# Expert chunks four at a time: evidence products in five blocks, PSUM banks by number

## The chip, the cores and the metric

One Trainium2 chip; the kernel runs on one of its cores, in one launch. The metric is device time in microseconds (us), as the median of several runs. Engines are named as the profile names them: PE (TensorE, matrix products), DVE (VectorE), ACT (ScalarE), POOL (GpSimd) and SP (SyncE, which here only issues transfers).

## The reference, cut to what matters

Eight samples of 512 tokens with 256 features. Everything is float32.

```python
nx = layer_norm(x) * ln_gamma + ln_beta                  # (8, 512, 256)
k, v = context @ Wk, context @ Wv                         # (8, 64, 256)
weights = softmax(nx @ Wq @ k.T / 16)                     # (8, 512, 64)
evidence = weights @ v                                    # (8, 512, 256)
combined = concat([nx, evidence, anchor])                 # (8, 512, 768)
probs = softmax(combined @ router_W + router_b)           # 3 experts
h = silu(combined @ e_w1[e] + e_b1[e])                    # 512 wide, each e
routed = sum_e probs_e * (h_e @ e_w2[e] + e_b2[e])
g = sigmoid(silu(combined @ gate_w1 + gate_b1) @ gate_w2 + gate_b2)
out = x + g * (routed @ out_w + out_b)
```

## The kernel before

The samples are worked on in four pairs, `j` = 0 to 3. Tokens lie on the free side: an activation is a tile of 128 features by 512 tokens, and one such tile fills one PSUM bank.

**The first layer.** Its 14 chunks of 128 outputs (12 of three experts, 2 of the gate) form seven groups of two chunks, `GROUPS`: group 0 is the gate's, 1 and 2 are expert 0's, 3 and 4 expert 1's, 5 and 6 expert 2's. For each group the four outputs of a 2x2 problem (two chunks times the two samples of the pair) are computed with seven products in place of eight, on sums and differences of the operands (`ws`, `T`, `combine_x`). They gather in three banks, U, Y and Z. By the numbers that the changed code gives them they are: 1 opens U; 2 goes to Y; 5 and then 3 go to Z; 6, 7 and 4 go to U. Between them partial sums have to be taken out: U after 1 and after 6 and Z after 5 by an ACT copy, U after 7 and Y after 2 by a DVE addition. A product that adds to a bank waits for the copy or addition that reads it. `silu` on ACT makes the four outputs; the last of them read U and Z when all is in.

**The evidence's part.** The term `evidence @ W` is added as `vw^T wT` with a contraction of only 64 rows (64 context positions). Two such products, one for each sample, use the upper and the lower 64 rows of PE. `evidence(j, n)` issues a block of them: one for U of group n-2, one for Z of n-1, one each for Y and Z of group n.

**Weighing.** Each expert chunk is multiplied by its router probability on DVE (`weigh`, line 714, tile `pb`, four per group), and one subtraction per group prepares the second layer (line 711). They are put in a list, `late`, and `weigh` takes a fixed number off it at fixed places.

**The second layer and the gate** are in `outputs(j, steps)`: the gate's seven products (`ps_gu`, `ps_gy`, `ps_gz`), then seven runs of six products over the chunks, with the subtractions of line 843, the bias sums (ACT 848, DVE 852) and the final sums (872 to 875). Steps of the next pair are put between them: transposes of its tokens, scores and softmax, `value_weights`, the router. One small detour matters here: a 3-row piece of `vw` is written to DRAM (`vrd`, line 331, POOL's queue) and read back on all partitions (`vr`, line 333); `router_logits` (lines 570 to 583, DVE) multiplies with it.

In pair 0 the preparation of the weights is spread over the first layer as well: `anchor_rows` and `anchor_columns` (biases from the condition), `second_bias`, and for every expert `transpose_second` (DVE, line 402), `second_layer` (PE, line 410, the product of e_w2 and out_w) and `combine_second` (POOL).

The order on every engine is written out by hand (`manual_schedule`): each queue runs in the order in which the code issues, and `put` places the steps. PSUM's eight banks come from four pools: two banks for U, one for Y, two for Z and three (`misc`) that rotate for everything else.

Of the kernel before, what the change touches and what calls it, by code (L numbers as in the profile page):

```python
# [16 lines left out]
def kernel(  # L17
# [74 lines left out]
    ps_x = ctx.enter_context(tc.tile_pool(name="ps_x", bufs=2, space=PSUM))  # L92
    ps_y = ctx.enter_context(tc.tile_pool(name="ps_y", bufs=1, space=PSUM))
    ps_z = ctx.enter_context(tc.tile_pool(name="ps_z", bufs=2, space=PSUM))
    ps_m = ctx.enter_context(tc.tile_pool(name="ps_m", bufs=3, space=PSUM))

    def misc(name):
        return ps_m.tile([P, 512], F32, tag="m", name=name)

    def bank(pool, name):  # L100
        return pool.tile([P, 512], F32, tag="b", name=name)
# [136 lines left out]
    def either(name):  # L238
        turn[0] += 1
        return bank((ps_x, ps_z)[turn[0] % 2], name)  # L240
# [400 lines left out]

    GROUPS = (NE // 2, *range(NE // 2))
    U, Z, Y = {}, {}, {}
# [5 lines left out]
    def take_banks(j, n):  # L649
        Y[n], Z[n] = bank(ps_y, f"ps_y_{j}_{n}"), bank(ps_z, f"ps_z_{j}_{n}")  # L650

    def evidence(j, n, start=True):

        wT, vw = S["wT", j], S["vw", j]
        todo = []
        if n - 2 in U:
            todo.append((U[n - 2], 2 * GROUPS[n - 2] + 1, 0, False))
        if n - 1 in Z:  # L660
            todo.append((Z[n - 1], 2 * GROUPS[n - 1], 1, False))
        if n < len(GROUPS):
            if n:
                take_banks(j, n)
            todo.append((Y[n], 2 * GROUPS[n], 0, start))
            todo.append((Z[n], 2 * GROUPS[n] + 1, 1, start))
        for ps, c, i, first in todo:
            half = slice(i * CT, (i + 1) * CT)
            product(ps, vw[half, c * P : (c + 1) * P], wT[half, :], start=first)
# [5 lines left out]
    def silu(j, n, i, d, src):  # L675
        c = 2 * GROUPS[n] + d
        nc.scalar.activation(  # L677
            chunk(n, i, d), src, AF.Silu, bias=abias[:, c, 2 * j + i : 2 * j + i + 1]
        )

    def add_silu(j, n, i, d, part, more):
        h = chunk(n, i, d)
        nc.vector.tensor_tensor(h, more, part, ALU.add)  # L683
        silu(j, n, i, d, h)

    def fourth(j, n):
        c = 2 * GROUPS[n]
        product(U[n], w1[:, 1, (c + 1) * P : (c + 2) * P], S["T", j][:, 2, :])
# [3 lines left out]

    late = []

    def weigh(j, n, most=8):


        for m, d, i in ((n - 1, 1, 0), (n, 0, 0), (n, 0, 1), (n, 1, 1)):
            if 0 < m < len(GROUPS):
                late.append((m, d, i))  # L700
        if 0 < n < len(GROUPS):
            late.append((n, None, None))
        if ("pb", j) in S and (j or n > 2):
            weigh_late(j, most)

    def weigh_late(j, most):
        for m, d, i in late[:most]:
            q = GROUPS[m]
            if d is None:
                b12 = hidden(j, q, 0, 1)  # L710
                nc.vector.tensor_tensor(b12, b12, hidden(j, q, 0, 0), ALU.subtract)
            else:
                h = hidden(j, q, d, i)
                nc.vector.tensor_tensor(h, h, S["pb", j][:, i, 2 * q // RC, :], ALU.mult)  # L714
        del late[:most]

    def first_layer(j, n, steps, last_steps):
        q = GROUPS[n]
        c, g = 2 * q, 2 * q // RC
        if c % RC == 0:  # L720
            for i in range(2):
                S["h", i, g] = h_tile(i, g, f"h_{2 * j + i}_{g}")
        A, Bx = S["nxT", 2 * j], S["nxT", 2 * j + 1]
        t1, t2, t3 = S["T", j][:, 0, :], S["T", j][:, 1, :], Bx[:, 0, :]
        ca, cb = chunk(n, 0, 0), chunk(n, 1, 0)
        U[n] = bank(ps_x, f"ps_u_{j}_{n}")
        product(U[n], w1[:, 0, c * P : (c + 1) * P], A[:, 0, :], start=True)
        first = j == n == 0
        if n == 0:
            take_banks(j, 0)  # L730
        if first:
            anchor_columns(E, either)
            anchor_columns(0, either)
            transpose_w(0)
        elif n == 0:
            evidence(j, 0)
        nc.scalar.copy(ca, U[n])  # L737
        if n:
            silu(j, n - 1, 1, 1, chunk(n - 1, 1, 1))
        product(Y[n], w1[:, 1, c * P : (c + 1) * P], A[:, 1, :], start=first)  # L740
        product(Z[n], ws[:, S1, q, :], t1, start=first)
        if first:
            evidence(j, 0, start=False)
        z = work.tile([P, T], F32, tag="z", name=f"z_{j}_{n}", bufs=1)
        nc.scalar.copy(z, Z[n])
        add_silu(j, n, 0, 0, Y.pop(n), ca)
        for step in steps:
            step()
        if n == 1:
            b12 = S["h", 1, E][:, 0, :]  # L750
            nc.vector.tensor_tensor(b12, b12, S["h", 0, E][:, 0, :], ALU.subtract)
        weigh(j, n - 1)
        if n:
            fourth(j, n - 1)
        product(U[n], ws[:, S2, q, :], t2)
        nc.scalar.copy(cb, U[n])
        product(Z[n], ws[:, S4, q, :], Bx[:, 1, :])
        evidence(j, n + 1)
        if n:
            silu(j, n - 1, 0, 1, U.pop(n - 1))  # L760
        add_silu(j, n, 1, 0, Z.pop(n), cb)
        product(U[n], w1[:, 0, (c + 1) * P : (c + 2) * P], t3)
        nc.vector.tensor_tensor(chunk(n, 1, 1), z, U[n], ALU.add)  # L763
        for step in last_steps:
            step()

    def finish_first_layer(j):
        n = len(GROUPS) - 1
        fourth(j, n)
        evidence(j, n + 2)  # L770
        silu(j, n, 0, 1, U.pop(n))

    def outputs(j, steps):
# [7 lines left out]
        silu(j, len(GROUPS) - 1, 1, 1, chunk(len(GROUPS) - 1, 1, 1))  # L781
        weigh(j, len(GROUPS) - 1, 99)
# [4 lines left out]
        def scratch_x(tag, bufs=1):  # L787
            return work.tile([P, T], F32, tag=tag, name=f"g_{tag}_{j}", bufs=bufs)

        def minus(dst, p, m):  # L790
            nc.vector.tensor_tensor(dst, p, m, ALU.subtract)
# [7 lines left out]
        t2, t3, t4 = scratch_x("z"), scratch_x("yb", 2), scratch_x("yb", 2)  # L799
        g1, g2, g22 = scratch_x("r11"), scratch_x("r12"), scratch_x("r22")  # L800
        y, z, u = (misc(f"ps_g{n}_{j}") for n in "yzu")
        product(u, gw[0][0], b11, start=True)
        nc.scalar.copy(g1, u)
        product(z, gw2s[:, S1, :], b12, start=True)
        nc.scalar.copy(g22, z)
        minus(t2, b22, b12)
        minus(t3, t2, b11)
        minus(t4, b21, t2)
        finish_first_layer(j)
# [9 lines left out]
        weigh(j, len(GROUPS), 99)  # L819
# [98 lines left out]
        u, y, z = (bank(p, f"ps_{n}2_{j}") for p, n in ((ps_x, "u"), (ps_y, "y"), (ps_z, "z")))  # L918
# [44 lines left out]
        y = bank(ps_z, "ps_y3")  # L963
# [5 lines left out]
    with tc.manual_schedule(engines=None):  # L969
# [56 lines left out]
        for j in range(NP):  # L1026


            within, ending, between = {}, {}, {}
# [4 lines left out]
            if j == 0:  # L1034
                put(within, 0, value_weights, 0, 1)
                put(ending, 0, router_logits, 0)
                put(within, 1, router_logits, 1)
                put(within, 1, anchor_rows, 1)
                put(within, 1, load_second, 1)
                put(within, 1, second_bias)  # L1040
                for b in range(2):
                    put(within, 2, router_exp, b)
                    put(ending, 2, router, b)
                put(within, 2, anchor_columns, 1)
                put(within, 2, load_second, 2)
                put(within, 2, transpose_second, 0)
                put(ending, 2, second_layer, 0)
                put(ending, 2, spread_probabilities, 0)
                put(ending, 2, combine_second, 0)
                put(within, 3, anchor_rows, 2)  # L1050
                put(within, 3, transpose_second, 1)
                put(ending, 3, second_layer, 1)
                put(ending, 3, combine_second, 1)
                put(ending, 3, weigh_late, 0, 5)
                put(within, 4, anchor_columns, 2)
                put(within, 4, transpose_second, 2)
                put(ending, 4, second_layer, 2)
                put(ending, 4, combine_second, 2)
            if j:
                put(ending, 0, spread_probabilities, j)  # L1060
            put(within, 1 + (j == 0), value_weights, j, 2)
            put(within, 4, load_x_blocks, 2 * j)
            put(within, 6, load_x_blocks, 2 * j + 1)
            if j + 1 < NP:
# [5 lines left out]
                for i in range(2):  # L1070
                    put(within, 3, deviation, j + 1, i)
# [62 lines left out]
```

## Time and profile before

| | |
|---|---|
| median of 3 runs | 488.87 us (488.67 to 489.21) |
| the profiled execution's own time | 489.28 us |
| its span, first to last instruction | 487.5 us |
| mean granted PE clock | 1.00 |
| DVE busy | 349.1 us (72%) |
| ACT busy | 219.1 us (45%) |
| PE's longest wait for another engine after the set-up | 0.87 us (line 647 for DVE line 763, at 54.5 us) |

The profile lists instructions by line of the kernel, with the tiles they write and read (numbers left out: `ps_u` is U of every group). One float32 product shows as two MATMUL records. PE's records are pipelined and overlap: the time of a product is the distance between starts, not the duration of a record. In the timeline "x2" merges neighbours of the same kind, and what stands in brackets is the idle time before the instruction and what ended it.

### The profile page before, as it was taken

Reading aid. Unit: us, or ns where it says so; the run is one execution under the profiler, and the core shown is the slowest. Engines: PE = TensorE matmul, PEld = TensorE weight load, DVE = VectorE, ACT = ScalarE, POOL = GpSimd, SP = SyncE. Lnnn points to the kernel's source line nnn. Section 1 sums busy time; section 2 is a strip of 40 time slices with the busy share of each in tenths; the row PEclk is TensorE's granted clock in tenths of the full one; section 3 lists DMA queues with packets and bytes.
Section 4 is the critical chain, followed back from the end, with each engine's and each line's share of the span. In section 5 each row is a group of like instructions: output and inputs, shape, how many; then the busy total and the mean of one; then the engine's idle time right before and its main releaser. Section 6 shows DMA issues by size and latency. Waiting matters only on the chain.

```text
span 487.5 us, 4704 instructions
## 1 busy us (share of the span) xinstructions
PE 481.2 (99%) x1451; PEld 222.5 (46%) x1451; DVE 349.1 (72%) x649; ACT 219.1 (45%) x391; POOL 77.2 (16%) x96
## 2 busy tenths in 40 slices
PE   8999999999999999999999999999999999999997
PEld 7744355535544434335544343434554343433454
DVE  2855748887879476878869575878879645668782
ACT  3463573468120648467210547567311455556000
POOL 5327032200242100000062200000042200000010
PEclk9999999999999999999999999999999999999999
DMA  9987331512002740612002740432002560000013
GB/s 283 377 110 144 57 131 44 108 22 44 0 16 43 163 142 0 143 30 43 1 17 43 158 144 1 118 56 44 2 16 43 81 180 0 0 0 2 0 19 68
DMA packets 118121, 35.27 MB, mean 72 GB/s; under 512 B 104733, under 2 KB 115089, under 8 KB 117585
## 3 DMA queue, kind: packets, MB, share of 16 engines
q1 hardware_dynamic: 114736, 27.02, 26.4%
q0 software_dynamic: 1472, 7.18, 4.3%
q10 hardware_dynamic: 1888, 0.79, 0.6%
q8 instruction: 11, 0.18, 0.2%
q14 instruction: 14, 0.11, 0.1%
HBM read 27.57 MB, written 7.40 MB: 72 GB/s over the span
## 4 chain that ended last, share of the span: by engine, by line
PE 84%; DMA 6%; ACT 3%; DVE 3%; issue 2%; POOL 1%; DVEq 0%; ACTq 0%; POOLq 0%
PE ps_u L647 39%; PE ps_z L647 18%; PE ps_y L647 12%; PE ps_vw L625 4%; PE ps_gu L647 3%; DMA w<-in_L_xcond_e_w_dram 2%; PE ps_s L525 2%; PE ps_w2o L410 2%; DMA vr<-vrd 2%; PE ps_gz L647 1%; DMA w<-in_L_xcond_gate_w_dram 1%; DVE h L843 1%; ACT h L677 1%; PE ps_gy L647 1%; DMA scr_w<-in_L_xcond_Wk_dram 1%
## 5 line engine op out<-in xcount | busy, mean ns | idle before, releaser
L677 ACT ACTIVATE h<-h,abias 128x512 f32<-128x512 f32 x84 | 60.7, 723 | 28.2 <-DVE h L683 25.9
L647 PE MATMUL ps_u<-h,w2o 128*128 128x512 f32 x144 | 63.8, 592 | 0.0
L714 DVE TENSOR_TENSOR h<-h,pb 128x512 f32<-128x512 f32 x96 | 60.0, 683 | 0.0
L647 PE MATMUL ps_u<-nxT,w 128*128 128x512 f32 x112 | 57.8, 621 | 0.3
L647 PE MATMUL ps_z<-wT,vw 64*128 64x512 f32 x112 | 56.5, 619 | 0.0
L647 PEld LDWEIGHTS ps_u<-h,w2o 128*128 128x128 f32 x144 | 27.4, 190 | 34.0 <-issue 33.9
L647 PE MATMUL ps_z<-h,w2s 128*128 128x512 f32 x96 | 42.6, 593 | 0.2 <-DVE r L858 0.2
L875 POOL TENSOR_TENSOR yb<-yb,xb 128x512 f32<-128x512 f32 x14 | 21.8, 1555 | 129.2 <-DVE yb L874 124.9
L683 DVE TENSOR_TENSOR h<-h,ps_y 128x512 f32<-128x512 f32 x28 | 19.2, 687 | 28.6 <-PE ps_y L647 23.0
L683 DVE TENSOR_TENSOR h<-h,ps_z 128x512 f32<-128x512 f32 x28 | 19.1, 684 | 20.1 <-PE ps_z L647 12.8
L647 PEld LDWEIGHTS ps_u<-nxT,w 128*128 128x128 f32 x112 | 18.4, 189 | 32.7 <-issue 17.2
L763 DVE TENSOR_TENSOR h<-z,ps_u 128x512 f32<-128x512 f32 x28 | 19.2, 687 | 19.4 <-PE ps_u L647 19.4
L677 ACT ACTIVATE h<-ps_u,abias 128x512 f32<-128x512 f32 x28 | 19.2, 687 | 30.1 <-PE ps_z L647 25.2
L647 PE MATMUL ps_u<-wT,vw 64*128 64x512 f32 x56 | 31.4, 641 | 0.0
L843 DVE TENSOR_TENSOR h<-h,h 128x1024 f32<-128x1024 f32 x24 | 31.0, 1347 | 0.0
L737 ACT COPY h<-ps_u 128x512 f32<-128x512 f32 x28 | 16.4, 584 | 31.8 <-PE ps_u L647 18.1
L647 PE MATMUL ps_u<-T,w 128*128 128x512 f32 x56 | 28.9, 598 | 0.9 <-DVE h L763 0.9
L647 PE MATMUL ps_y<-wT,vw 64*128 64x512 f32 x56 | 29.3, 604 | 0.0
L647 PE MATMUL ps_y<-nxT,w 128*128 128x512 f32 x56 | 28.9, 598 | 0.0
L647 PE MATMUL ps_z<-nxT,ws 128*128 128x512 f32 x56 | 28.9, 597 | 0.0
L647 PE MATMUL ps_u<-T,ws 128*128 128x512 f32 x56 | 28.6, 592 | 0.0
L647 PE MATMUL ps_z<-T,ws 128*128 128x512 f32 x56 | 28.6, 592 | 0.0
(197 smaller groups left out, 764.4 us busy)
## 6 DMA issues: line engine op xcount, KB each, us to landing
pb<-pd POOLq DMA_DIRECT2D x4, 1536.0 KB, 6.5
x<-in_x_dram SPq DMA_DIRECT2D x8, 512.0 KB, 5.5
xb<-in_x_dram SPq DMA_DIRECT2D x64, 64.0 KB, 2.5
out_dram<-yb SPq DMA_DIRECT2D x56, 64.0 KB, 2.0
w<-in_L_xcond_e_w_dram SPq DMA_DIRECT2D x6, 512.0 KB, 9.4
xd<-x SPq DMA_DIRECT2D x6, 512.0 KB, 2.8
xg<-xd SPq DMA_DIRECT2D x48, 64.0 KB, 2.5
scr_wa<-in_L_xcond_e_w_dram SPq DMA_DIRECT2D x3, 512.0 KB, 5.5
```

What stands on the lines that cost most here:

```text
L410: nc.tensor.matmul(ps[:, d * H : (d + 1) * H], w2T[:, k, (i + d) * P : (i + d + 1) * P], ow_sb[:, k, :], start=(k == 0), stop=(k == KH - 1),)
L525: nc.tensor.matmul(ps[:, t, :], nxT[:, k, t * P : (t + 1) * P], mr[:, k, b, :], start=(k == 0), stop=(k == KH - 1),)
L625: nc.tensor.matmul(ps, vT[:, k, j * 2 * CT : (j + 1) * 2 * CT], w1[:, KH + k, n0:n1], start=(k == 0), stop=(k == KH - 1),)
L647: nc.tensor.matmul(ps, lhsT, rhs, start=start, stop=True, skip_group_check=not start)
L677: nc.scalar.activation(chunk(n, i, d), src, AF.Silu, bias=abias[:, c, 2 * j + i : 2 * j + i + 1])
L683: nc.vector.tensor_tensor(h, more, part, ALU.add)
L714: nc.vector.tensor_tensor(h, h, S["pb", j][:, i, 2 * q // RC, :], ALU.mult)
L737: nc.scalar.copy(ca, U[n])
L763: nc.vector.tensor_tensor(chunk(n, 1, 1), z, U[n], ALU.add)
L843: nc.vector.tensor_tensor(d, p, m, ALU.subtract)
L875: nc.gpsimd.tensor_tensor(yb, yb, S["xb", 2 * j + row][:, i, :], ALU.add)
```

## The change

The gate's group is done first by itself (`gate_layer`), then each expert's two groups together (`expert_layer`), with their products alternating. The evidence's products are issued in one block at the end of each of these, and one for the gate's group at its start: five blocks for each pair of samples. The banks are taken by number; `spares` says which banks `misc` may rotate over at a place. The partial sums wait in the `h` chunks themselves. The gate's differences (`gate_differences`, before in `outputs`) move into expert 2's layer, and the steps of `put` get new places.

```diff
-    ps_x ... bufs=2, ps_y ... bufs=1, ps_z ... bufs=2, ps_m ... bufs=3
+    psum = ctx.enter_context(tc.tile_pool(name="psum", bufs=1, space=PSUM))
+    def bank(i, name):
+        return psum.tile([P, 512], F32, tag=f"b{i}", name=name)
     def misc(name):
+        spare.append(spare.pop(0))
+        return bank(spare[-1], name)
+    spares(4, 6, 7)
...
+    PAIRS = [(1 + 2 * e, 2 + 2 * e) for e in range(E)]
+    Z_BANKS = ((5, 7), (0, 2), (5, 7))
+    def fresh(j, e):
+        for n, y, z in zip(PAIRS[e], (4, 6), Z_BANKS[e]):
+            Y[n], Z[n] = bank(y, ...), bank(z, ...)
...
+    def gate_layer(j, steps):
...
+        U[n] = bank(0, f"ps_u_{j}_{n}")
+        nx_product(j, n, 1, True)
+        Y[n], Z[n] = bank(5, f"ps_y_{j}_{n}"), bank(2, f"ps_z_{j}_{n}")
...
+            evidence(j, ((n, True),))
+        spares(3, 1)
+        keep_part(n, 0, 0, U[n])
+        nx_product(j, n, 5, first)
...
+        keep_part(n, 1, 1, Z[n])
+        nx_product(j, n, 6)
+        keep_part(n, 1, 0, U[n])
+        if not first:
+            nx_product(j, n, 2)
...
+        fresh(j, 0)
+        evidence(j, [(m, True) for m in PAIRS[0]] + [(n, False)])
...
+    def expert_layer(j, e, steps):
+        a, b = PAIRS[e]
...
+        if e:
+            finish_groups(j, PAIRS[e - 1])
...
+        U[a] = bank(1, f"ps_u_{j}_{a}")
+        nx_product(j, a, 1, True)
+        keep_part(a, 0, 0, U[a])
...
+        U[b] = bank(3, f"ps_u_{j}_{b}")
+        nx_product(j, b, 1, True)
...
+        finish_odd(j, PAIRS[e - 1] if e else (0,))
+        if e > 1 or e and j:
+            weigh(j, 5)
+        spares(*Z_BANKS[1 - e % 2])
+        nx_product(j, a, 2)
+        add(a, 0, 0, Y[a])
+        nx_product(j, a, 5)
+        keep_part(a, 1, 1, Z[a])
+        run("A")
+        nx_product(j, a, 6)
...
+        nx_product(j, b, 6)
...
+        nx_product(j, b, 2)
...
+        nx_product(j, b, 5)
...
+        spares(*Z_BANKS[1 - e % 2], 4, 6)
+        run("B")
+        for n in (a, b):
+            nx_product(j, n, 7)
+            add(n, 1, 1, U[n])
...
+        if e:
+            weigh(j, 6)
+        run("C")
...
+        for n in (a, b):
+            nx_product(j, n, 3)
+        run("D")
+        for n in (a, b):
+            nx_product(j, n, 4)
+        if e + 1 < E:
+            fresh(j, e + 1)
+            evidence(j, [(m, False) for m in (a, b)] + [(m, True) for m in PAIRS[e + 1]])
+        else:
+            evidence(j, [(m, False) for m in (a, b)])
...
     def outputs(j, steps):
-        silu(j, len(GROUPS) - 1, 1, 1, chunk(len(GROUPS) - 1, 1, 1))
-        weigh(j, len(GROUPS) - 1, 99)
...
+        u, z, y = (bank(i, f"ps_g{n}_{j}") for n, i in (("u", 0), ("z", 2), ("y", 4)))
         product(u, gw[0][0], b11, start=True)
+        product(z, gw2s[:, S1, :], b12, start=True)
+        finish_groups(j, PAIRS[-1])
         nc.scalar.copy(g1, u)
+        finish_odd(j, PAIRS[-1])
         nc.scalar.copy(g22, z)
-        minus(t2, b22, b12)
-        minus(t3, t2, b11)
-        minus(t4, b21, t2)
-        finish_first_layer(j)
+        spares(6, 7, 4)
...
         run("begin")
-        weigh(j, len(GROUPS), 99)
+        weigh(j, 99)
...
-        u, y, z = (bank(p, ...) for p, n in ((ps_x, "u"), (ps_y, "y"), (ps_z, "z")))
+        u, y, z = (bank(i, f"ps_{n}2_{j}") for i, n in ((1, "u"), (3, "y"), (5, "z")))
...
+                put(within, (0, "A"), router_logits, 1)
+                put(within, (0, "A"), anchor_rows, 1)
+                put(within, (0, "A"), load_second, 1)
+                put(within, (0, "B"), second_bias)
...
+                put(within, (1, "A"), transpose_second, 1)
+                put(within, (1, "B"), second_layer, 1)
+                put(within, (1, "B"), combine_second, 1)
+                put(within, (1, "C"), anchor_columns, 2)
+                put(within, (1, "C"), transpose_second, 2)
+                put(within, (1, "D"), second_layer, 2)
+                put(within, (1, "D"), combine_second, 2)
-                put(ending, 3, weigh_late, 0, 5)
...
+            put(within, (0, "C" if j == 0 else "B"), value_weights, j, 2)
+            put(within, (1, "C"), load_x_blocks, 2 * j)
+            put(within, (2, "A"), gate_differences, j)
+            put(within, (2, "C"), load_x_blocks, 2 * j + 1)
...
+                put(within, (0, "A"), statistics, b0, 0, NT)
+                put(within, (0, "C" if j else "D"), statistics, b1, 0, NT)
+                put(within, (1, "C"), deviation, j + 1, i)       # for i in 0, 1
+                put(within, (1, "D"), normalize, b0)
+                put(within, (2, "C"), normalize, b1)
+                put(within, (2, "C"), store_x, b1)
```

In the new functions `keep_part` is the ACT copy of a partial sum into its `h` chunk, `add` the DVE addition, `finish_groups` the SiLU from U and the addition of Z for two groups, `finish_odd` the SiLUs after that addition. `nx_product(j, n, which)` issues the product with that number.

## The prediction

> **What bounds the kernel now.** I read the page's busy times first, then PE's timeline around an evidence block, then the other engines' timelines at the places where a step moves.
>
> ```profile
> PE 481.2 (99%) x1451; PEld 222.5 (46%) x1451; DVE 349.1 (72%) x649; ACT 219.1 (45%) x391; POOL 77.2 (16%) x96
> ```
>
> PE is busy for 481 of 487.5 us: PE's order sets the time, a product taken out is time gained, a PE wait is time lost. PE's timeline shows what a product and a block cost:
>
> ```profile
> 170.88 1.02 PE L647 MATMUL ps_z<-nxT,ws 128*128 128x512 f32 x2
> 171.83 0.69 PE L647 MATMUL ps_u<-wT,vw 64*128 64x512 f32 x1
> 171.84 0.69 PE L647 MATMUL ps_z<-wT,vw 64*128 64x512 f32 x1
> 172.37 0.59 PE L647 MATMUL ps_u<-wT,vw 64*128 64x512 f32 x1
> ...
> 173.75 1.55 PE L647 MATMUL ps_u<-nxT,w 128*128 128x512 f32 x3
> ```
>
> Starts of records inside a run are 0.429 apart, so a product (two records) takes 0.858. Two evidence products run side by side (171.83 and 171.84) and take 0.858 together. Entering the block costs 0.09 more, its second step 0.10, leaving it 0.10, the first product behind it 0.10: 0.40 for each block. A block of one pair of products spans 2.115 between its neighbours, one of two pairs 2.973: one pair, 0.858, more. So the 0.40 is per block, not per pair.
>
> The other view is the hand-over between two pairs of samples (here j=1 to j=2), where DVE, not PE, has no room:
>
> ```profile
> 223.61 0.67 DVE L503 STREAM_TRANSPOSE nxT<-xg 128x512 f32<-128x512 f32 x1
> 224.20 0.65 DVE L714 TENSOR_TENSOR h<-h,pb 128x512 f32<-128x512 f32 x1
> 226.57 2.87 DVE L852 SCALAR_TENSOR_TENSOR r<-pb,b2o,r 128x512 f32<-128x512 f32 x4 [1.72 <-ACT r L848]
> 230.65 0.17 DVE L537 COPY lg<-ps_s 128x12 f32<-128x12 f32 x1
> ```
> ```profile
> 234.04 0.78 POOL L331 DMA_DIRECT2D vrd<-vw  x1 [62.95 <-ACT vw L632]
> 243.87 0.55 POOL L333 DMA_DIRECT2D vr<-vrd  x1 [9.06 <-DMA vrd<-vw]
> ```
> ```profile
> 248.01 0.69 DVE L570 TENSOR_TENSOR pv<-w,vr 128x384 f32<-128x384 f32 x1 [4.23 <-DMA vr<-vrd]
> 251.65 0.42 DVE L550 TENSOR_TENSOR w<-w,rs 128x256 f32<-128x256 f32 x1
> ...
> 268.45 0.93 DVE L873 TENSOR_TENSOR r<-r,h 128x512 f32<-128x512 f32 x1
> ```
> ```profile
> 269.49 0.58 ACT L737 COPY h<-ps_u 128x512 f32<-128x512 f32 x1 [4.12 <-DVE r L873]
> ```
> ```profile
> 270.38 1.02 PE L647 MATMUL ps_z<-T,ws 128*128 128x512 f32 x2
> 271.24 1.02 PE L647 MATMUL ps_u<-T,ws 128*128 128x512 f32 x2
> ```
>
> This is one chain: one weigh, then the bias sums (852), the scores' maxima and logits (to 537), ACT's exponentials and its copy of `vw`, POOL's 9 us through DRAM, the landing at 248.0, and from there DVE without a gap to the last sum at 269.4. Only then may ACT's copy overwrite `h`, and only then may PE put product 6 into U. Before has 1.1 us of room there (copy done 270.07, product 6 at 271.24).
>
> **The blocks.** Before issues nine blocks for each pair of samples (two products short of full pairs: 15 slots of 0.858), after five blocks in 14 slots. Per pair of samples 4 x 0.399 + 0.858 = 2.454, times four: **-9.82**. No block of before has three or four pairs; the two sizes it has differ by exactly a pair, so I extrapolate. If the overhead grew with the pairs instead, only the slots would be won (3.43) and the time would be 6.4 higher; the rows exclude that. Products of two groups alternate between banks, as U, Y and Z do now at 0.429: nothing.
>
> **Waits that go.** PE waits for the addition behind product 7 or the copy of Z before it may reuse a bank: 1.03 at 53.0 (0.87 of it on the page's line for 647), 0.22 each at 57.2, 190.5 and 301.9, three of 0.09. With two groups alternating, each of these has a product or more between: **-1.95**. The steady layers have no other: an expert's layer takes PE 14 x 0.858 + 4 x 0.858 + 0.40 = 15.84, DVE some 11 and ACT some 9.5 (0.60 for a DVE operation, 0.62 for a SiLU, 0.48 for a copy, start to start), so nothing new is late inside them.
>
> **New waits in pair 0.** DVE's order there:
>
> ```profile
> 46.03 0.69 DVE L683 TENSOR_TENSOR h<-h,ps_y 128x512 f32<-128x512 f32 x1
> 46.63 0.55 DVE L570 TENSOR_TENSOR pv<-w,vr 128x384 f32<-128x384 f32 x1
> ...
> 49.56 0.28 DVE L353 COPY ar<-ps_ar 128x128 f32<-128x128 f32 x1
> ```
>
> `second_bias` now follows `anchor_rows` with the rotation over banks 0, 2, 4, 6 set anew, so `ps_b2o` takes bank 0, the bank of the second `ps_ar`; it waits for DVE's copy of that. PE is there at 48.5. DVE gets `vr` at 42.56 as now, ends the first router logits at 46.03, adds twice (1.2), does the second logits (2.93) and the copy (0.28): 50.45. **+2.0**; all of PE's queue stands behind it. The DVE transposes of `transpose_second(0)` cost `second_layer(0)` **+0.15**.
>
> In expert 1's layer `second_layer(2)` stands in "D" behind `transpose_second(2)` in "C". On DVE there are, between the addition of group 4's product 7 and those two transposes, six operations of `weigh(j, 6)` (6 x 0.602 = 3.61), the bias addition, and the transposes (two in 1.30 by their row, 79.43). On PE there lie only `pt_ab` and two products, 1.83. From the addition's end that is 3.6 + 0.2 + 1.3 + the hand-overs (0.1 each) against 1.83: PE stands from 80.6 to 84.3 of its own new time, **+3.7**. Now the weighs of pair 0 come after the transposes (82.12), so nothing waits.
>
> Is a 3.7 us stand of PE itself a danger? The first products of the run (128 columns) start 0.213 apart from 1.06 to 6.2 us and 0.109 later; the same slowness after the stand would cost up to 2.6. The longest PE wait of before after the set-up, 1.03, has nothing slow behind it, so I take nothing and keep 2.6 for the upper end. [...]
>
> **The hand-overs.** Before takes 8 operations at a time off the weighing list in each of seven layers and has one left at "begin", behind the transposes of the next tokens (503). After takes 5 and 6 off per expert layer, and its last two groups are finished only then: 13 (j=0) or 8 (j=1 to 3) stand between the transposes and the bias sums. Those are due 0.60 apart. j=0: 112.85 + 13 x 0.602 = 120.68 in place of 115.22, **5.46 later**; j=1, 2: 224.20 + 8 x 0.602 = 229.02 in place of 226.57, **2.45 later** each (the 1.72 us in which DVE waited for ACT are already used). The chain above passes this on: exponentials, `vw`, 9 us of DRAM and 4.1 to the landing, then 21 us of DVE without a gap. PE has some room of its own: product 6 comes one slot earlier now (270.38), the copy ends at 270.07, so 0.3. In j=0 the loss shows in parts (runs of the second layer about 2.7, `pt_w` 1.9, product 6 1.0), in j=1 and 2 `pt_w` about 1.2 and product 6 about 1.0. 5.5 + 2.2 + 2.2: **+9.9**. Below, this could be nothing if the slack were elsewhere; above, the DRAM round can be 0.9 longer (4.96 against 4.1 for the landing).
>
> **At no cost.** `gate_differences` (four operations, 2.4) goes into expert 2's layer where DVE idles between 3.7 and 6.2 of the layer; 2.4 per pair if that cover is gone. `value_weights(j, 2)` (1.72 of PE) only moves. On SP the store of the odd sample's tokens goes behind eight 64 KB loads (2.5 us each to land, in parallel); the transposes that need it come some 19 us later. The last pair ends as before, **+0.05**.
>
> **The sum.** -9.82 - 1.95 + 2.0 + 0.15 + 3.7 + 9.9 + 0.05 = +4.0 on the profiled 489.28 (0.41 above the median of 488.87): 493.3, as a median **492.9**. What a measurement of this kernel can tell from no change is about 0.2%, 1 us.
>
> **The rivals.**
> - *As summed*, 492.9, its own range 489.5 to 496. For it: the queue orders and the unbroken DVE stretch. 0.63.
> - *The hand-overs absorb the delay* (the other side). If DVE or ACT makes up the 5.5 and 2.2 before `pt_w` and product 6, the 9.9 is not paid: 492.9 - 9.9 = **483.0**. The change turns into a gain once the hand-overs cost under 5.9 together. For it: DVE is idle for 4.2 us just ahead of 248.0 and does fewer gate subtractions there. Against: that idle time waits for the DRAM round, whose start is what is late. 0.19.
> - *No new wait at all*: 488.87 - 11.77 = **477.1**. Against it stand two orders that can be counted. 0.05.
> - *More than summed*: slow products behind the stand (+2.6) or DVE stretched beside POOL (a line-843 subtraction took 2.29 in place of 1.2): 495.5 to **497**. 0.13.
> - That the blocks do not merge is excluded by the order of the products.
>
> The range 482.5 to 497.0 takes in the first two cases and most of the last; the chances are 0.24 faster, 0.04 the same, 0.72 slower (the second and third case are faster; 0.04 of the first I put near no change).
>
> **What would show it.** 20 evidence blocks in place of 36; PE waits for DVE at `ps_b2o` (2 us near 50) and at `ps_w2o` (3.7 near 84); 13 or 8 weighs ahead of the bias sums; `vr` landing some 5.5 and 2.4 later behind the transposes; PE waiting at `pt_w` and at product 6. It is wrong if those waits are not there, or if a block of four pairs shows more than 0.4.

## The result, and the profile after

The changed kernel takes **493.93 us** (493.74 to 494.81, 4 runs) against 488.77 for the kernel before, measured beside it: 1.0108 times as long (95% interval 1.009 to 1.0125). The forecast was 492.9 with a range of 482.5 to 497.0. The profiled execution took 494.81 us, the sum had said 493.3. On another chip, in a later comparison, the same kernel took 497.03 (495.73 to 500.59), 1.0175 times as long (1.0143 to 1.0208): it scatters far more than the kernel before, and two of the experiments show why. One execution of the experiment with the transposes first, its profiled one, ran at a mean granted clock of 0.95 (501.51 us) and is left out of every comparison.

The page after, PE's busy time and the granted clock over the 40 slices:

```profile
span 493.0 us, 4641 instructions
...
PE 474.7 (96%) x1451; PEld 224.7 (46%) x1451; DVE 347.2 (70%) x649; ACT 218.1 (44%) x391; POOL 77.7 (16%) x96
...
PEclk9999998899999999999999999999999999999999
```

PE is busy 6.5 us less than before, and the span is 5.5 us longer: PE now waits. Two slices show a clock below full. PE's waits by what ended them (us in total, times, longest):

```profile
PE ps_w2o L416 <- DVE scr_w2T L408: 4.4, 1, 4.4
PE pt_w L564 <- DVE w L556: 2.0, 3, 1.0
PE ps_u L656 <- ACT h L691: 2.0, 3, 0.7
PE ps_b2o L437 <- DVE ar L359: 1.5, 1, 1.5
PE ps_u L656 <- DVE h L923: 1.2, 1, 1.2
PE ps_u L656 <- DVE h L732: 1.1, 1, 1.1
```

Every line is one that the forecast named: the transposes behind the weighs, the hand-over's `pt_w` and product 6 (three each), `ps_b2o`, and two in pair 0's second layer. The old line for the addition behind product 7 is gone. The greatest of them in PE's timeline, and the clock around it (for each stretch: its length, the busy us of PE, PEld, DVE, ACT and POOL with their counts, then the granted clock, the DMA share and GB/s):

```profile
78.35 1.88 PE L656 MATMUL ps_z<-nxT,ws 128*128 128x512 f32 x4
84.59 6.36 PE L416 MATMUL ps_w2o<-ow_sb,scr_w2T 128*128 128x256 f32 x16 [4.36 <-DVE scr_w2T L408]
90.78 1.45 PE L656 MATMUL ps_u<-T,w 128*128 128x512 f32 x3
```
```profile
78.00:84.50 6.50, 2.23 (x6) 0.68 (x4) 6.22 (x11) 3.71 (x6) 2.66 (x4) 0.90 0.00 0
84.50:90.00 5.50, 5.41 (x13) 4.33 (x14) 2.07 (x7) 0.59 (x1) 0.00 (x0) 0.50 0.27 95
```

Sixteen records that take 3.5 us at full clock (those of expert 1, from 73.07 to 76.53) lie between 84.59 and 90.78, 6.2 us: the clock is 0.50 from 83.14, still in the wait, to 89.96. This was the forecast's upper end (2.6), not its centre.

The hand-over from pair 1 to 2, DVE's and POOL's timelines, where before had one weigh between the transposes and the bias sums:

```profile
229.90 1.30 DVE L509 STREAM_TRANSPOSE nxT<-xg 128x512 f32<-128x512 f32 x2
231.12 1.85 DVE L732 TENSOR_TENSOR h<-h,pb 128x512 f32<-128x512 f32 x3
...
235.54 0.69 DVE L729 TENSOR_TENSOR h<-h,h 128x512 f32<-128x512 f32 x1
236.15 2.73 DVE L932 SCALAR_TENSOR_TENSOR r<-pb,b2o,r 128x512 f32<-128x512 f32 x4
```
```profile
243.31 0.78 POOL L337 DMA_DIRECT2D vrd<-vw  x1 [64.25 <-ACT vw L638]
252.36 0.56 POOL L339 DMA_DIRECT2D vr<-vrd  x1 [8.28 <-DMA vrd<-vw]
```

From the first weigh to the bias sums it is 5.03 us (before: 2.37), to the issue of `vrd` 12.19 (before: 9.84). The DRAM trip then took 13.4 in place of 14.0, so the logits started 25.57 behind the first weigh in place of 23.81.

### The profile page after: what moved, and what is told of

Its sections match the earlier page's. It is cut to its first block, busy times and chain, and to the rows that moved or that the text cites. A ratio compares the mean times of both kernels' runs of the same rounds, so it can differ in the third digit from the quotient of the medians.

```text
span 493.0 us, 4641 instructions
## 1 busy us (share of the span) xinstructions
PE 474.7 (96%) x1451; PEld 224.7 (46%) x1451; DVE 347.2 (70%) x649; ACT 218.1 (44%) x391; POOL 77.7 (16%) x96
## 4 chain that ended last, share of the span: by engine, by line
PE 36%; issue 28%; DVE 20%; DMA 11%; ACT 3%; POOL 2%; DVEq 0%; POOLq 0%; ACTq 0%
PE ps_u L656 17%; PE ps_z L656 7%; PE ps_y L656 6%; DVE h L923 4%; DMA vr<-vrd 4%; DVE pv L576 3%; PE ps_w2o L416 3%; DMA w<-in_L_xcond_e_w_dram 2%; DVE r L953 2%; DVE le L582 2%; DMA vrd<-vw 2%; DVE r L952 2%; DVE h L732 2%; DMA w<-in_L_xcond_gate_w_dram 1%; DVE yb L954 1%
## 5 line engine op out<-in xcount | busy, mean ns | idle before, releaser
L732 DVE TENSOR_TENSOR h<-h,pb 128x512 f32<-128x512 f32 x96 | 61.7, 692 | 10.0 <-ACT h L682 10.0
L682 ACT ACTIVATE h<-h,abias 128x512 f32<-128x512 f32 x84 | 58.0, 719 | 17.4 <-DVE h L688 16.9
L656 PE MATMUL ps_u<-nxT,w 128*128 128x512 f32 x112 | 55.4, 605 | 0.0
L691 ACT COPY h<-ps_u 128x512 f32<-128x512 f32 x56 | 32.7, 584 | 47.7 <-PE ps_u L656 35.3
L656 PE MATMUL ps_z<-wT,vw 64*128 64x512 f32 x112 | 53.3, 608 | 0.0
L337 POOL DMA_DIRECT2D vrd<-vw x4 | 3.2, 796 | 166.3 <-ACT vw L638 166.3
L576 DVE TENSOR_TENSOR pv<-w,vr 128x384 f32<-128x384 f32 x16 | 15.0, 938 | 20.3 <-DMA vr<-vrd 20.0
L656 PEld LDWEIGHTS ps_z<-h,w2s 128*128 128x128 f32 x96 | 18.1, 190 | 22.3 <-issue 19.9
L656 PE MATMUL ps_u<-wT,vw 64*128 64x512 f32 x56 | 27.8, 611 | 0.0
L688 DVE TENSOR_TENSOR h<-h,ps_u 128x512 f32<-128x512 f32 x28 | 18.7, 685 | 12.8 <-PE ps_u L656 12.3
```

The lines of the kernel that those rows point to most:

```text
L576: nc.vector.tensor_tensor(pv, w[:, t : t + NT // 2, :].unsqueeze(2).to_broadcast(list(pv.shape)), vr.unsqueeze(1).to_broadcast(list(pv.sha ...
L656: nc.tensor.matmul(ps, lhsT, rhs, start=start, stop=True, skip_group_check=not start)
L682: nc.scalar.activation(h, h if src is None else src, AF.Silu, bias=abias[:, c, 2 * j + i : 2 * j + i + 1])
L688: nc.vector.tensor_tensor(h, h, part, ALU.add)
L691: nc.scalar.copy(chunk(n, i, d), part)
```

## The experiments

All of them start from the changed kernel. "Beside" means a kernel before in the same comparison (488.9 to 489.5 in all four). The kernels of different groups ran on different chips, so ratios are compared across groups, times within one.

### One cause for the stall and the slow products?

**Transposes first.**

```diff
-    if e: weigh(j, 6)
-    run("C")                     # (1, "C") holds transpose_second(2)
+    run("before C")              # holds transpose_second(2)
+    if e: weigh(j, 6)
+    run("C")
```

> The changed kernel with one move: expert 2's two DVE transposes stand before the six weighs in expert 1's layer of pair 0. My theory: the wait of ps_w2o for DVE (4.5 us) and the slow products behind it (13 records 0.213 too long, 2.8) have this one cause, so both go: 493.9 - 7.4 = 486.5 us, and the records of ps_w2o are 0.216 apart. DVE can pass the gain on, because it idles 7.2 us (for PE) between there and the hand-over. Rival: DVE is the bound of pair 0 and the hand-over takes it back: 490 or more, with longer waits at the hand-over to pair 1.

Measured: 1.0019 times the kernel before (1.0003 to 1.0035), about 489.8. Against the changed kernel's 1.0108 and 1.0175 this gains 4.4 to 7.6 us. It is 3.3 short of the 486.5 forecast and at the rival's figure, and no trace of a comparable execution says where the rest went; the same move is measured on a quieter base at the end of this section.

**The wait filled.** In `second_layer(2)`, in front of the first product:

```diff
+    for _ in range(5):
+        product(ps, w1[:, 0, :P], S["nxT", 0][:, 0, :], start=True)
```

> The changed kernel with five useless products (4.29 us, their sum is overwritten) put into the 4.5 us in which PE waits for expert 2's transposes. Clock theory: the transposes come no earlier, but PE does not stand idle, so the products of ps_w2o run 0.216 apart instead of 0.427: 493.9 - 2.8 = 491.1 us. Rival (the products are slow for a reason of their own, as a read of a tile that DVE has just written, or DVE and POOL at work beside them): 493.9, records still 0.427 apart. Second rival: useless products delay what follows: over 494.

Measured: 493.86 (493.21 to 494.82), ratio 1.0104. The theory's mechanism is in the trace, PE's clock before and behind the same arrival of the transposes:

```profile
78.00:84.00 6.00, 6.00 (x16) 2.58 (x14) 5.73 (x10) 3.53 (x6) 2.54 (x3) 1.00 0.00 0
84.00:88.50 4.50, 4.43 (x18) 3.25 (x18) 2.39 (x7) 0.76 (x2) 0.00 (x0) 1.00 0.26 94
```

The same products at the same place run at 1.00 in place of 0.50 when PE had work before them: here the idle time slowed them, not the fresh tile. The forecast time missed by 2.8: PE was 2.7 us ahead of the changed kernel's profile at 88, and only 1.3 at its last product. Between them `pt_w` waited 1.40, 1.23 and 1.26 in the three hand-overs, against 1.13, 0.60 and 0.79, beside DRAM trips of 13.7, 13.8 and 13.7 us against 13.0, 13.4 and 13.0.

**The wait shortened.** `weigh(j, 3)`, the transposes, `weigh(j, 3)`.

> The changed kernel with expert 2's transposes after three of the six weighs: the wait of PE becomes 4.5 - 3 x 0.602 = 2.7 us. If only a wait above some length between 2.7 and 4.5 us slows the clock, the slow records vanish with it: 493.9 - 1.8 - 2.8 = 489.3 us. If any wait of some us slows it, the records stay 0.427 apart: 492.1 us.

Measured: 493.63 (491.85 to 495.09), ratio 1.0094, above both forecasts. In its trace the wait was 2.50 and no record of `ps_w2o` behind it was at half clock (granted clock 1.00 from 78 to 88). But here the clock fell somewhere else, behind the 1.48 us wait for `ps_b2o`, where the changed kernel's first profile shows none:

```profile
48.00:52.00 4.00, 2.69 (x13) 1.53 (x12) 3.73 (x16) 1.47 (x3) 0.00 (x0) 0.97 0.73 115
52.00:56.00 4.00, 4.00 (x23) 1.62 (x22) 3.44 (x15) 2.32 (x4) 0.00 (x0) 0.60 0.20 31
```

The 2.0 us of wait and the 2.7 us of slow products that are gone are mostly taken back: some 1.7 by this slow stretch and 1.7 by longer `pt_w` waits (1.57, 1.51 and 1.15).

So a length of wait alone does not decide: 2.50 went without, 1.48 did not, and in the changed kernel's first profile the 1.65 for `ps_b2o` went without too (1.00 from 48 to 56). The slow stretches differ in length: 6.83 us in that profile (83.14 to 89.96), some 3.4 here, worked out from the 0.97 and 0.60 of the two stretches above. PE's busy time around a wait goes with the fall in one pair of places and not in another. From 78.00 to 84.50 in the changed kernel's first profile PE was busy for 2.23 of 6.50 us, and the clock fell; from 78 to 84 here, with the 2.50 in it, for 3.81 of 6.00, and it did not. From 48 to 52 PE was busy for 2.69 of 4.00 us here, and the clock fell; in the first profile for 2.52 of 4.00, and it did not. What decides was not shown.

### The bank of `ps_b2o`

The rotation in expert 0's layer is set to banks 2, 0, 4, 6 in place of 0, 2, 4, 6.

> The changed kernel with the rotation of banks in expert 0's layer starting at bank 2 instead of 0, so that ps_b2o does not take the bank of the second ps_ar. My theory: the wait of ps_b2o for DVE line 359 (1.65 us between starts) goes and nothing takes its place, since DVE idles 4.4 us for PE before the next wait: 493.9 - 1.65 = 492.3 us. Rival: DVE sets the pace of pair 0, and the 1.65 comes back in the wait of ps_w2o (6.2 instead of 4.5): 493.9 us.

Measured: 495.83 (495.54 to 496.16), ratio 1.0143, so no gain that shows, and neither forecast is met. In the trace the wait is gone, but 0.24 (for `ps_vw`) and 0.65 (for `ps_w2o` of expert 0) of it come back within 8 us, both for DVE, which has no gap there. The rest, 0.76, is about what the set-up differed between the two profiles (0.69 later at the first scores), and the wait for expert 2's transposes is 4.5 as before. Why the time is longer, by 1.7 us going by the ratios, this run does not settle; its `pt_w` waits, 1.6 longer in all (1.41, 1.19, 1.49), stand beside longer DRAM trips again (13.9, 13.6, 13.7).

### The weighs of the hand-over

Four kernels on one chip: the changed kernel again, the late weighs moved, three moves together, and those with split blocks.

> The changed kernel itself, unaltered, beside the others: 493.9 us if nothing but its own order sets it; up to 495.5 if the trip of the logits' piece of vw through DRAM (13.0 to 13.9 us from its write's issue to its landing in the traces so far) is 0.5 longer on this chip at each of the three hand-overs, since every part of it is then PE's wait.

Measured: 497.03, ratio 1.0175, above the forecast's upper end. In its profiled execution (500.51) the trips took 14.3, 14.0 and 14.2 us, and `pt_w` waited 1.93, 1.70 and 1.70 against 1.13, 0.60 and 0.79 in the first profile; the clock fell behind `ps_b2o` too (0.65 from 50 to 54 us). These two account for 2.8 and 1.7 of the 5.7 us between the two profiles; 0.7 of the rest lies in the set-up and 0.6 behind the last product. Between these two executions a longer trip was a longer wait of PE at each of the three hand-overs, and the wait for `ps_b2o` brought a slow stretch in one and not in the other.

```diff
-    weigh(j, 99)                                  # behind "begin"
+    weigh(j, 99 if last else 0 if j else 5)
...
     put(between, "P1", scores, b0)
+    put(between, "P1", weigh, j, 99)
```

> The changed kernel with the late weighs moved on DVE's queue: for pairs 1 and 2 all eight, for pair 0 eight of thirteen, behind the bias sums and the next pair's score maxima. My theory (the weighs ahead of the bias sums delay the DRAM trip, and that delay is the hand-over's loss): the chain starts 4.1 and about 2 us earlier, the waits for pt_w and for product 6 go and those of pair 0 in the second layer too, 7.6 in all of which I expect 7: 486.9 us. Rival (the loss is elsewhere: the trip itself or DVE's 21 us behind its landing): the waits stay, 493 us or more. Second rival: the weighs then come late for the second layer's own products: waits of ps_z or ps_u for DVE line 732 or 923, 489 to 492 us.

Measured: 497.46 (494.41 to 501.56), ratio 1.0163: nothing gained. The mechanism is the second rival's, but the time is 5 us above its figure. No `pt_w` and no product 6 waits any more, so the weighs were what delayed them. But the second layer waited in their place, at all three hand-overs:

```profile
PE ps_u L656 <- DVE h L923: 3.6, 3, 1.2
PE ps_b2o L437 <- DVE ar L359: 2.0, 1, 2.0
PE ps_z L656 <- DVE h L729: 1.9, 3, 0.6
```

In the profiled execution (501.56) the granted clock is 0.983 over 499.8 us. If every slow stretch is at 0.50, that is an estimated 17 us at half clock, up to 8.5 lost, against 7 us in the changed kernel's first profile (0.993 over 493.0).

> The changed kernel with three moves: expert 2's transposes before the six weighs, ps_b2o in bank 2, and the late weighs behind the score maxima. If the three losses are separate: 493.9 - 7.4 - 0.7 - 7 = 478.8 us, close to the blocks' and old waits' gain alone (477.1). If DVE is the bound of pair 0, which takes back what one move gives: 482 to 486 us.

Measured: 490.03 (488.07 to 494.09), ratio 1.0033 (1.0006 to 1.006), above both forecasts. The stall of 4.5 is gone and the two new waits at each hand-over stay. In the profiled execution (494.09, the longest of twelve) the granted clock is 0.989 over 492.3 us, by the same estimate 11 us at half clock; others of the twelve have a granted clock of 0.997 to 1.0 and take 488 to 490 us. At the hand-over of pair 0, PE and clock:

```profile
124.18 1.12 PE L656 MATMUL ps_z<-h,w2s 128*128 128x512 f32 x2 [0.64 <-DVE h L729]
126.50 5.83 PE L656 MATMUL ps_u<-h,w2s 128*128 128x512 f32 x9 [1.20 <-DVE h L924]
```
```profile
120.00:124.00 4.00, 3.55 (x9) 1.28 (x7) 3.93 (x7) 1.99 (x10) 0.81 (x1) 1.00 0.04 4
124.00:127.00 3.00, 1.62 (x3) 0.79 (x4) 3.00 (x5) 1.52 (x2) 0.00 (x0) 0.92 0.00 0
127.00:131.00 4.00, 4.00 (x7) 1.52 (x6) 4.00 (x5) 0.00 (x0) 0.00 (x0) 0.63 0.00 0
```

Two waits, 0.80 and 1.36 between starts, cost 2.2 us, and the slow stretch behind them (0.92, then 0.63) some 1.7 again.

> The kernel with the three moves, and the evidence block behind experts 0 and 1 cut in two (one pair of products goes between the layer's two last products): 8 more blocks in all, the same products. If a block costs 0.40 whatever its length: 8 x 0.40 = 3.2 us longer than the kernel with the three moves. If the cost is per pair of products or nothing: the same as that.

Measured: 492.46 (491.55 to 493.68), 2.4 longer than without the split, on a base that scatters by 6 us. It is repeated below on a quieter one.

### The waits taken out, and put back one at a time

The traces say where DVE has room: 4.4 us in pair 0's expert 1 layer, some 1 us before each of the gate's first two additions, and 2.3 us behind the next tokens' transposes, where it waits for ACT's bias sums. The weighs go there, each chunk's second operand first:

```diff
+    if e == 1 and not j: weigh(j, 5)              # ahead of run("B")
+    run("before C")                               # transposes, then weigh(j, 6)
...
-    weigh_rest(n)                                 # for a, then for b
+    late.extend([(a, 1, 1), (b, 1, 1), (a, 0, 1), (a, 1, 0), (a, None, None)])
+    late.extend([(b, 1, 0), (b, None, None), (b, 0, 1)])
...
+    weigh(j, 1)
     gate(0, 0, g1, y)
     product(z, gw2s[:, S4, :], b22)
+    weigh(j, 1)
     gate(0, 1, g2, z)
...
-    weigh(j, 99)
+    weigh(j, 99 if last else 4)                   # rest behind the score maxima
```

In pair 0 also: banks 2, 0, 4, 6; `transpose_second(0)` ahead of the router, and the first statistics moved from "A" to "C".

> The changed kernel with its blocks untouched and only DVE's queue (and the bank of ps_b2o) set anew: expert 2's transposes before the six weighs; five weighs of pair 0 in expert 1's layer where DVE idles 4.4 us; of the last eight weighs one before each of the gate's first two additions, four behind the next tokens' transposes, two behind the score maxima; in pair 0 one pair of statistics and the router behind the transposes of expert 0. My theory (the blocks' gain is real and all that hides it are waits of PE and the slow clock behind them): no PE wait over 0.5 us after the set-up, clock 1.00, near 488.9 - 11.8 = 477.1; I expect 477 to 480 us. Rival (DVE has no room, each move makes another wait): 484 us or more.

Measured: **479.18 us** (478.6 to 480.78), 0.9802 times the kernel before (0.9784 to 0.982): below both kernels. All of PE's waits in its trace:

```profile
PE ps_wake L255 <- DVE warm_t L158: 1.1, 1, 1.1
PE ps_ar L354 <- ACT w L546: 0.2, 1, 0.2
PE ps_u L656 <- ACT h L691: 0.2, 1, 0.2
PE ps_s L531 <- DVE mr L318: 0.2, 1, 0.2
PE ps_z L656 <- DVE r L944: 0.2, 1, 0.2
```

The clock is 1.00. The forecast's rival of no new wait stood at 477.1; it is reached to about 2 us once the waits are really taken out.

> The same kernel with the last eight weighs ahead of the bias sums again, as in the changed kernel: the hand-over alone, at 8 weighs in each pair of samples. By the waits of the changed kernel at pairs 1 and 2 (0.6 to 1.7 for pt_w and 0.82 for product 6): 3 x (1.4 to 2.5) = 4.2 to 7.5 us more than the kernel with the waits taken out. If the order of the weighs does not matter: the same as that.

Measured, beside it on the same chip: 486.37 (485.51 to 486.98), 7.2 us more. Its waits are the hand-over's and no others:

```profile
PE pt_w L564 <- DVE w L556: 5.2, 3, 2.2
PE ps_u L656 <- ACT h L691: 2.0, 3, 0.7
```

The edit moves only weighs on DVE's queue. That settles the hand-over: with all eight weighs between the transposes and the bias sums, in place of the four that about fill DVE's wait there, each of three hand-overs costs 2.4 us.

> The kernel with the waits taken out, with one thing put back: expert 2's transposes behind the six weighs of expert 1's layer. PE then waits 3.6 us or more for them (six weighs at 0.60, up to 4.5 when POOL works beside them), and if such a wait halves the clock for 3.4 us or more, 1.5 to 3 us are lost on top: 5.3 to 7.5 us more than 479.2. If the wait alone costs and the clock stays: 3.7 to 4.5 more. If a later slack takes it back: under 3 more.

Measured: 485.87 (485.24 to 487.04), ratio 0.9935 (0.9916 to 0.9953), 6.7 us more than with the waits out (their ratios differ by 0.0133, 6.5 us). The trace has the wait and the clock behind it:

```profile
PE ps_w2o L416 <- DVE scr_w2T L408: 4.3, 1, 4.3
```
```profile
77.00:83.00 6.00, 1.67 (x4) 0.38 (x2) 5.93 (x10) 3.15 (x6) 2.16 (x3) 1.00 0.00 0
83.00:86.00 3.00, 2.99 (x7) 2.43 (x8) 1.99 (x6) 0.00 (x0) 0.00 (x0) 0.51 0.01 2
```

The wait is 4.5 between starts, and the sixteen products behind it take 5.02 us in place of 3.30, 1.7 more; 0.5 is left open. Together the two things put back account for 13.9 of the 14.8 us between the changed kernel and this one (13.3 of 15.0 by the ratios). The wait for `ps_b2o` and the other moves in pair 0 were not put back alone.

> The kernel with the waits taken out, with the evidence block behind experts 0 and 1 cut in two: 8 more blocks, the same products. If a block costs 0.40 whatever its length: 479.2 + 3.2 = 482.4 us. If the cost goes with the pairs of products: 479.2.

Measured: 482.41 (481.78 to 483.04), ratio 0.9856 (0.9837 to 0.9875): 3.2 us more for eight blocks by the medians, 2.6 by the ratios, as the two kernels ran on different chips. The traces give the price itself: blocks of one, two, three and four pairs span 2.115, 2.973, 3.832 and 4.690, each pair 0.858 more, so a block carries the same 0.40 at each of these four lengths.

## Why the prediction held, step by step

Against the profiled execution (494.81, 5.5 above before's):

| step | forecast | in the profile after |
|---|---|---|
| blocks and the slot | -9.82 | 20 blocks; four pairs 4.690, as extrapolated: 0.40 for each block |
| old PE waits | -1.95 | gone (the one put at 57.2 stood at 59.4) |
| `ps_b2o` behind `anchor_rows` | +2.0 | +1.65 |
| `second_layer(0)` | +0.15 | under 0.1 |
| `second_layer(2)` behind six weighs | +3.7 | +4.52 |
| slow products behind it | 0, with 2.6 as upper end | +2.7 |
| hand-overs | +9.9 | +7.62 (10.4 in the repeat) |
| last pair's end | +0.05 | 0.8 more from the last product's start to the end; not explained |

The order of the kernel was read rightly: which instruction stands ahead of which, and who waits for it, decided every entry but the last. That the total came within 1.5 us of the profile is partly luck: the stall and the clock cost 3.5 more than forecast and the hand-overs 2.3 less. In the repeat the hand-overs were near their forecast, and the median, 497.03, lay at the upper edge of the range. The sizes that were off are these.

- The stall. The six weighs were priced at 0.602; two of them took 1.04 and 1.21, beside POOL's last operations of `combine_second(1)`. The forecast kept this stretching for one of its rivals, not for this place.
- The clock. I took nothing because no wait of before was followed by slow products. The longest of those was 1.03, so the row could not say anything of 4.5; the case for zero was weak, and 2.6 was the better row. This is the mis-sized step. In the profile the clock was 0.50 for 6.83 us, and the products behind the wait took 2.7 more.
- The hand-overs. The delay on DVE was right (the bias sums start 2.66 later behind the first weigh, forecast 2.45). I let the DRAM trip be as long as before's 14 us or longer; in the first profile it was 13.0 to 13.4, in the repeat 14.0 to 14.3, and PE's loss went with it, 7.6 and 10.4. The range should have opened to both sides here.

The rival on the other side, hand-overs that absorb the delay, is refuted by the kernel with the eight weighs put back: 7.2 us for nothing but their place in DVE's queue.

## What to carry to other kernels

Taking work from the engine that is 99% busy pays only as far as the others can deliver for the shorter schedule: write down, for each queue, what now stands ahead of the operation that the busy engine will wait for, above all where a long chain through DRAM starts. The same list shows where the queue idles, and moving the small operations there turned a loss of 5 us into a gain of 10. A wait of the busy engine costs more than its length when its clock falls behind it: 2.7 us on top of 4.52 here. Three kernels whose granted clock differs from one execution to the next (0.989 to 0.996, 0.983 to 0.993, 0.989 to 1.0) scatter by 5 to 7 us; the one with the waits taken out (0.998 to 1.0) by 2.2.

## What was not expected of the hardware

- TensorE's clock also fell behind waits much shorter than the 3.7 us that the prediction asked about. Behind 4.5 us it was 0.50 from 84.5 to 90 in the changed kernel's first profile, 0.50 from 87 to 92 in its repeat and 0.51 from 83 to 86 with the stall put back. Behind 2.50 us it stayed at 1.00 (78 to 88). Around `ps_b2o`: 1.00 from 48 to 56 with 1.65 us, 0.65 from 50 to 54 with 1.57 in the repeat, 0.60 from 52 to 56 with 1.48. Behind 0.80 and 1.36 us in close succession: 0.63 from 127 to 131. Behind three waits of up to 2.2 us for `pt_w`, with no other wait over 0.7 after the set-up, no fall shows: 0.998 over the whole execution with the eight weighs put back. So much the same wait brought a fall in one execution and not in another; why was not shown.
- A trip of a three-row piece through DRAM, from the issue of its write to its landing on all partitions, took 13.0 to 14.3 us in the same kernel from run to run. In the kernel before, with trips of 14.0 to 14.3, PE never waited for `pt_w`; in the changed one it waited 0.60 to 1.13 with trips of 13.0 to 13.4, and 1.70 to 1.93 with 14.0 to 14.3.
